# A gated cross-attention kernel: the preparation of its first attention becomes a stream of the timetable, and the loads are put in order of first use

## The chip, the core and the metric

The kernel runs on one core of a Trainium2 chip. The core has a matrix engine (TensorE, PE in the profile, with PEld for its weight loads), a vector engine (VectorE, DVE), a scalar engine (ScalarE, ACT), a general engine (GpSimd, POOL) and a sync engine (SyncE, SP) that here only starts DMA transfers. Each engine runs its own queue of instructions in order; engines wait for one another through semaphores. SBUF is the on-chip memory with 128 partitions, and PSUM is the memory of eight banks that TensorE writes to. The metric is device time in microseconds, lower is better.

## The reference

The input x has 16 batches of 256 tokens of 128 numbers, and the context has 64 tokens of 128 numbers for each batch. Four blocks follow one another, each added to x with a gate tanh(g):

1. a cross attention of x on the context with 16 heads of 8 numbers, causal, under a padding mask, with weights Wq, Wk, Wv and Wo and no biases;
2. two layers of a local-attention network: token shift, 8 heads of 64, rotary position, windows of 64, then a gated GELU network;
3. a second cross attention with biases and another mask;
4. a mixture of 8 experts with the two best of each token.

```python
x = x + tanh(g_xattn[0]) * L0_xattn(layernorm(x), ctx, ctx, mask_if1, Wq, Wk, Wv, Wo)
x = x + tanh(g_ffn[0])   * L0_ffn(layernorm(x), ...)
x = x + tanh(g_xattn[1]) * L1_xattn(layernorm(x), ctx, ctx, mask_ik0, ...)
x = x + tanh(g_ffn[1])   * L1_ffn(layernorm(x), ...)
# L0_xattn: Q = q @ Wq.T; K = k @ Wk.T; V = v @ Wv.T
# scores = where(causal and mask, Q K^T / sqrt(8), -inf); softmax(scores) @ V @ Wo.T
```

## The kernel before

The kernel holds x in SBUF as `x_sb`, 32 tiles of 128 tokens, two tiles to a batch, and works batch by batch. There are three stages: the first cross attention, the local network with both layers, and the second cross attention together with the experts. Inside a stage the order of instructions on every engine comes from `play`, which follows `timetable`. That function plays through tables of steps such as `CROSS_STEPS`: a row has the step's name, its lag (in which round of the loop a batch reaches it), its engine, an assumed duration, the steps it needs, and the buffers that it takes with the steps that give each back. Several tables can be played together as streams; a stream may wait for a step of another. On each engine a stream's steps keep the order given by lag and table row. The assumed durations only decide the order; on the chip the engines wait for one another through semaphores.

One batch of the first cross attention goes through these steps. DVE takes mean and variance (`stat`, L776), POOL the root and the normalised rows (`rstd`, `apply`, L781 to L794), PE turns the rows (`turn`, L756) and ACT copies them out (L805). PE makes the query (`query`, L854) and ACT copies it to `QT` (L860). POOL spreads the batch's keys by head (`keys`, `Kd`, L841). PE makes the scores (`score`, L869 to L885): a row of mask penalties `pen`, a causal part from `causal_g` and `query_g`, and the products. DVE takes the maxima (`top`, L894) and splits them into three narrow parts (`parts`, L903 to L911), which PE turns (`mturn`, L916). PE makes the scores again with keys on the partitions (`score_t`, L932 to L946) with the maxima subtracted, ACT takes the exponential (L956), PE mixes the values (`mix`, L969), ACT and DVE divide (L978 to L992), PE projects (`project`, L999) and DVE adds to `x_sb` (`add`, L1006). One PSUM bank M serves turn, query, mturn and project; three pairs of banks (BIG0 to BIG2) serve the scores.

Before the stage there is a preparation, written out in program order. Loads: ACT starts the context (512 KB), the eight weight matrices (64 KB each), the two small masks and the router, and SP starts x in four pieces, the gates, the masks spread over all partitions (512 KB each), the four small pieces of `fill_c`, and after these all other weights. The framework hands out eight DMA semaphores in turn to all loads, so a load is issued only when the load eight places earlier in the program has landed, and its engine stands still until then. POOL makes the identity, the constants, the causal mask and the local masks `lmask`, which only the second stage reads, and clears buffers. DVE makes `head_of`, `sel`, 16 copies of the causal mask, 8 copies of the identity (`query_g`) and the penalties. Then `prepare` (L625) turns the four weights, turns the context, makes all keys (L608) and all values (L614) of layer 0, and turns the penalties (L654), in eight PSUM banks of its own (pool `bank_prep`). The stage's pool takes the same banks afterwards, so its first turn (L756) waits until they are given back. The corresponding work for the second cross attention, `rest`, is already a stream: `TABLE_STEPS` from the fourth batch on, `REST_STEPS` at the stage's end.

Of the kernel before, what the change touches and what calls it, by code (L numbers as in the profile page):

```python
# [30 lines left out]
E = 8  # L31
# [8 lines left out]
CROSS_STEPS = """  # L40
stat 0 DVE 0.92 - sm:apply
project 6 PE 0.5 share M:add
mturn 3 PE 0.25 parts M:mturn_out
score 2 PE 1.25 query_out,keys BIG:top0 BIG:top1
exp1 4 ACT 1.08 score_t,exp0
vals 2 POOL 0.32 - V:mix
mturn_out 3 ACT 0.38 mturn mT:score_t
top0 2 DVE 1.2 score
apply 1 POOL 1.02 offset xn:turn
turn 1 PE 0.4 apply M:turn_out  # L50
turn_out 1 ACT 0.38 turn xnT:query
mix 4 PE 1.8 exp0,exp1,vals O:share
log 4 ACT 0.38 mix
rstd 0 POOL 1.03 stat
top1 2 DVE 1.2 score,top0
query 1 PE 0.6 turn_out M:query_out
parts 2 DVE 0.9 top0,top1 mp:mturn
query_out 1 ACT 0.39 query QT:score+score_t
inverse 4 ACT 0.38 log
exp0 3 ACT 1.08 score_t pT:mix  # L60
score_t 3 PE 1.2 mturn_out,query_out,keys BIG:exp0 BIG:exp1
offset 0 DVE 0.16 rstd
add 5 DVE 0.48 project
refine 4 DVE 0.84 inverse
keys 1 POOL 0.6 - Kd:score+score_t
share 4 DVE 0.43 refine oT:project
# [55 lines left out]

REST_STEPS = """
vals_out1 1 DVE 0.7 vals1
vals0 2 PE 0.98 wturn_out BIG:vals_out0
bo_out 1 DVE 0.25 bo
rw_out 0 DVE 0.2 rw
vals_out0 3 DVE 0.7 vals0
vals_out3 3 DVE 0.7 vals3
cols_out 0 DVE 0.35 cols  # L130
keys_out0 0 DVE 0.75 keys0,cols_out
rw 0 PE 0.15 - BIG:rw_out
vals_out2 0 DVE 0.7 vals2
wturn 0 PE 0.6 - BIG:wturn_out
cols 0 PE 0.15 - BIG:cols_out
keys_out1 3 DVE 0.75 keys1,cols_out
keys0 0 PE 0.95 wturn_out BIG:keys_out0
vals2 0 PE 0.98 wturn_out BIG:vals_out2
bo 0 PE 0.4 bias,wturn_out BIG:bo_out
vals1 0 PE 0.98 wturn_out BIG:vals_out1  # L140
keys1 5 PE 0.95 wturn_out BIG:keys_out1
wturn_out 1 ACT 0.62 wturn
vals3 4 PE 0.98 wturn_out BIG:vals_out3
bias 0 DVE 0.25 cols_out
# [3 lines left out]
seen 7 DVE 1.0 -  # L148
fill 6 DVE 1.2 -
tab0 3 DVE 0.5 -  # L150
tab1 0 DVE 0.5 -
tab3 2 DVE 0.5 -
tab2 1 DVE 0.5 -
# [131 lines left out]
def timetable(streams, room):  # L285
# [26 lines left out]
    def can_go(k, name, b, engine, now):  # L312
# [5 lines left out]
        for j, n in [(k, n) for n in needs] + across.get(name, []):  # L318
            span = streams[j][5]
            if b < span.start:  # L320
                continue
# [59 lines left out]
def flamingo_kernel(ctx: ExitStack, tc: tile.TileContext, a: dict, out: bass.AP):  # L381
# [30 lines left out]
    for i in range(4):  # L412
        nc.scalar.dma_start(w_nat[:, i, :], a[NATS[i]])
# [18 lines left out]
    for g in range(4):  # L432
        nc.sync.dma_start(fill_c[32 * g : 32 * g + 3, :], a["fill_parts"])
# [1186 lines left out]
```

## Time and profile before

| | us |
|---|---|
| median of 3 runs | 1177.72 (1176.37 to 1178.03) |
| the profiled execution | 1179.12 |
| its span, first to last instruction | 1177.2 |
| busy PE / PEld | 1086.2 / 787.4 |
| busy DVE / ACT / POOL | 941.4 / 730.9 / 631.4 |
| first stage, until the last PSUM copy of its steps ends (DVE, L692) | 155.4 |
| mean granted TensorE clock | 0.982 |

The span is what the profiler saw between the first and the last instruction; the execution took 1.9 us more. A row of instructions reads: start, duration of the group, engine, line, operation, out<-in and shapes, count, and in brackets how long the engine stood idle before and what released it. The chain of waits is followed back from the last instruction, and names for each stretch the engine and line that it hung on. The granted clock is the share of full speed at which TensorE was allowed to run. Lines are those of the kernel before; the changed file has other numbers.

### The profile page before, as it was taken

How to read it: one execution, taken by the hardware profiler on the slowest of the kernel's cores; microseconds unless marked ns; L12 is line 12 of the kernel's file. 1: busy time of each engine (PE TensorE's matmuls, PEld its weight loads, DVE VectorE, ACT ScalarE, POOL GpSimd, SP SyncE). 2: the span in 40 equal slices, each digit the busy share in tenths (PEclk: the TensorE clock that was granted, in tenths of full speed). 3: DMA queues.
4: the chain of work that ended last, by engine and by line, in shares of the span. 5: the costliest groups of instructions: out<-in, count | busy, mean ns of one | idle time of the engine just before them, and what ended most of it. 6: DMA issues, size and time to landing. Idle time of an engine off the chain costs nothing.

```text
span 1177.2 us, 28295 instructions
## 1 busy us (share of the span) xinstructions
PE 1086.2 (92%) x11264; PEld 787.4 (67%) x11264; DVE 941.4 (80%) x2103; ACT 730.9 (62%) x1408; POOL 631.4 (54%) x1079
## 2 busy tenths in 40 slices
PE   5899968999999999988999999999979999999997
PEld 3555535677677777755767766777645557999996
DVE  5787678999999956669999999856667884777777
ACT  1455526888888873346888888863326657455552
POOL 4344158999988852338888888833344551111110
PEclk9899989999999999999999999999999999999999
DMA  6300001111111100001111111100000000000000
GB/s 193 126 3 2 3 14 37 37 29 37 29 38 38 27 17 14 1 0 37 38 37 30 37 37 29 33 11 1 1 1 2 2 2 2 12 13 12 13 12 17
DMA packets 29516, 30.02 MB, mean 26 GB/s; under 512 B 4484, under 2 KB 22344, under 8 KB 29384
## 3 DMA queue, kind: packets, MB, share of 16 engines
q1 hardware_dynamic: 27112, 27.15, 9.1%
q8 instruction: 89, 1.46, 0.5%
q10 hardware_dynamic: 2272, 1.06, 0.3%
q14 instruction: 43, 0.35, 0.1%
HBM read 9.33 MB, written 2.10 MB: 10 GB/s over the span
## 4 chain that ended last, share of the span: by engine, by line
PE 71%; DVE 16%; ACT 6%; issue 4%; POOL 1%; DVEq 0%; ACTq 0%; POOLq 0%
PE QK L1121 8%; PE e_y L1508 7%; PE e_h_ps L1486 7%; PE po L969 5%; PE Ag L1375 4%; PE OB L1281 4%; PE TR L1269 4%; PE SC L1228 3%; PE VB L1151 3%; PE OB L1299 3%; PE TR L1200 3%; ACT pr L1251 3%; PE sT L946 3%; DVE mx L1237 3%; PE sc L885 2%
## 5 line engine op out<-in xcount | busy, mean ns | idle before, releaser
L1251 ACT ACTIVATE pr<-SC,mx,rn 128x128 f32<-128x128 f32 x512 | 185.5, 468 | 35.9 <-DVE mx L1242 35.8
L1121 PE MATMUL QK<-wqkv,hbuf 128*128 128x512 f32 x256 | 130.9, 635 | 19.7 <-DVE qn L1132 14.9
L1264 POOL TENSOR_TENSOR pr<-pr,rs 128x1024 f32<-128x1024 f32 x64 | 121.3, 1896 | 14.6 <-DVE rs L1259 11.4
L1516 DVE SCALAR_TENSOR_TENSOR x_sb<-e_y,e_comb,x_sb 128x128 f32<-128x128 f32 x256 | 89.1, 349 | 21.6 <-PE e_y L1508 13.7
L1498 ACT ACTIVATE e_h<-e_h_ps 128x1024 f32<-128x1024 f32 x48 | 49.2, 1025 | 77.2 <-PE e_y L1508 61.8
L1121 PEld LDWEIGHTS QK<-wqkv,hbuf 128*128 128x128 f32 x256 | 44.6, 193 | 78.1 <-issue 42.1
L894 DVE TENSOR_REDUCE nm<-sc 128x16 f32<-128x1024 f32 x64 | 74.7, 1210 | 21.6 <-PE sc L885 21.5
L1508 PE MATMUL e_y<-mw,e_h 128*128 128x128 f32 x768 | 91.8, 277 | 0.0
L1486 PE MATMUL e_h_ps<-e_xnT,mw 128*128 128x256 f32 x384 | 89.8, 383 | 0.3
L1508 PEld LDWEIGHTS e_y<-mw,e_h 128*128 128x128 f32 x768 | 89.2, 192 | 0.7
L1166 POOL TENSOR_TENSOR qn<-qn,u 128x512 f32<-128x512 f32 x64 | 81.3, 1271 | 10.5 <-DVE qn L1132 7.9
L1132 DVE TENSOR_TENSOR u<-QK,tab 128x1024 f32<-128x1024 f32 x64 | 76.8, 1200 | 10.6 <-ACT sq L1129 5.2
L1129 ACT ACTIVATE sq<-QK 128x1024 f32<-128x1024 f32 x64 | 65.9, 1030 | 29.7 <-DVE u L1132 9.3
L1258 DVE TENSOR_REDUCE rs<-pr 128x8 f32<-128x1024 f32 x64 | 77.5, 1211 | 7.9 <-ACT pr L1251 5.3
L1237 DVE TENSOR_REDUCE mx<-SC 128x8 f32<-128x1024 f32 x64 | 77.6, 1212 | 6.4 <-PE SC L1228 6.4
L1167 POOL TENSOR_TENSOR qn<-qn,u 128x512 f32<-128x512 f32 x64 | 81.6, 1275 | 0.0
L956 ACT ACTIVATE xpT<-sT,penT 128x1024 f32<-128x1024 f32 x64 | 69.5, 1114 | 19.0 <-PE sT L946 19.0
L1272 ACT COPY pT<-TR 128x1024 f32<-128x1024 f32 x64 | 64.4, 1007 | 24.1 <-PE TR L1269 24.1
L1132 DVE TENSOR_TENSOR qn<-QK,tab 128x1024 f32<-128x1024 f32 x64 | 77.6, 1213 | 1.1 <-ACT sq L1129 1.1
L1146 DVE TENSOR_REDUCE ss<-sq 128x16 f32<-128x1024 f32 x64 | 77.1, 1205 | 1.1 <-ACT sq L1129 1.1
L1486 PEld LDWEIGHTS e_h_ps<-e_xnT,mw 128*128 128x128 f32 x384 | 70.3, 190 | 10.9 <-DVE x_sb L1516 2.7
L1385 ACT ACTIVATE hhg<-Ag,cols 128x256 f32<-128x256 f32 x64 | 28.7, 472 | 72.8 <-PE Ag L1375 36.4
(215 smaller groups left out, 2648.0 us busy)
## 6 DMA issues: line engine op xcount, KB each, us to landing
vbuf<-vbuf SPq DMA_DIRECT2D x96, 128.0 KB
hbuf<-yT SPq DMA_DIRECT2D x32, 64.0 KB
out_dram<-x_sb SPq DMA_DIRECT2D x32, 64.0 KB
hbuf<-yT SPq DMA_DIRECT2D x32, 63.8 KB
wqkv<-in_L_ffn_wqkv_dram SPq DMA_DIRECT2D x2, 768.0 KB
mw<-in_L_ffn_w_dram SPq DMA_DIRECT2D x2, 768.0 KB
x_sb<-in_x_dram SPq DMA_DIRECT2D x2, 640.0 KB
w<-in_L_ffn_w_dram SPq DMA_DIRECT2D x2, 341.0 KB
```

What stands on the lines that cost most here:

```text
L1121: nc.tensor.matmul(ps[:, 512 * j : 512 * j + 512], lhsT=hbuf[b % 3][:, W + t * P : W + (t + 1) * P], rhs=wqkv[:, l, 512 * j : 512 * j + 51 ...
L1132: nc.vector.tensor_tensor(work(tag, b, t, [P, 2, LH, LD], 2, wp), live["QK", b, t].rearrange("p (q h d) -> p q h d", q=2, h=LH), tab[:, l, ...
L1146: nc.vector.tensor_reduce(ss, live["sq", b, t].rearrange("p (g d) -> p g d", d=LD), AX.X, ALU.add)
L1166: nc.gpsimd.tensor_add(qg[:, :, 0:32], qg[:, :, 0:32], ug[:, :, 32:64])
L1167: nc.gpsimd.tensor_add(qg[:, :, 32:64], qg[:, :, 32:64], ug[:, :, 0:32])
L1237: nc.vector.tensor_reduce(mx, live["SC", b, t].rearrange("p (g c) -> p g c", c=P), AX.X, ALU.max, negate=True,)
L1251: nc.scalar.activation(pr[:, g, :], live["SC", b, t][:, g * P : (g + 1) * P], AF.Exp, bias=live["mx", b, t][:, g : g + 1], scale=live["rn" ...
L1258: nc.vector.tensor_reduce(rs, live["pr", b, t], AX.X, ALU.add)
L1264: nc.gpsimd.tensor_tensor(pr, pr, rs, ALU.mult)
L1486: nc.tensor.matmul(ps[:, c * S : (c + 1) * S], lhsT=mw1[:, (4 * j + c) * P : (4 * j + c + 1) * P], rhs=live["xnT", b], start=True, stop=True,)
L1508: nc.tensor.matmul(y[:, e * D : (e + 1) * D], lhsT=live["h", b][:, c, t * P : (t + 1) * P], rhs=mw2[:, c, :], start=(c == cs[0]), stop=(c ...
L1516: nc.vector.scalar_tensor_tensor(xt, live[f"y{t}", b][:, e * D : (e + 1) * D], live["comb", b][:, t, e : e + 1], xt, ALU.mult, ALU.add,)
```

## The change

`prepare` becomes a table, `FIRST_STEPS`, with a function for each step, and is played together with the batches of the first cross attention in the same PSUM pool: its steps use the three BIG pairs and the bank O. Steps of the batches get a list of needs on it (`needs`); a third entry gives the batch from which a need holds, for which `can_go` gets two new lines. Rows on engines named LW, LC, LX, LM, LN, LP, LA and LD stand for loads and constants with an assumed time of landing and issue nothing. Weights are turned in pairs, Wk with Wq and Wv with Wo, for which the list `NATS` and the indices of Wq and Wv change. `CROSS_STEPS` keeps its steps and durations but has other lags and another order of rows.

The loads are in another order and other pieces. ACT starts only Wk, the context in two halves, and Wq. SP starts x in pieces of 2, 2, 4, 6, 8 and 10 tiles, the wide mask of the first attention in one piece for two batches and one for fourteen, the other weights, the small masks, and the rest as before. In program order of the built kernel SP's queue is: x of batch 0, the two gates, `parts_in`, the mask of batches 0 and 1, x of batch 1, Wv, the two small masks, x of batches 2 and 3, the rest of the mask, Wo, and then the remaining x, the other mask, the weights of layer 1 and the router. The four small loads into `fill_c` become one load of six numbers to every partition and three small DVE steps (`part`). The copies of the causal mask become 8 of twice the width on DVE (`late`), those of the identity go to ACT (`unit`), and the penalties are made by two wider instructions instead of four.

The local masks move from POOL's start into four steps `local0` to `local3` of `TABLE_STEPS`, after the fourth batch has begun its scores. `TABLE_STEPS` and `REST_STEPS` get new lags and row order.

In the built program the order of TensorE from the query of batch 2 to the stage's end is the old one, apart from the turn of the router weights, which moves three steps towards the end, and the last keys and values, which change places. Before that, TensorE's order is: Wk and Wq turned, both halves of the context, Wv and Wo, keys 0, batch 0 turned, values 0, query 0, penalties, values 1, scores 0, batch 1 turned, values 2, query 1, keys 1, values 3, mturn 0, scores 1. On DVE the add now stands ahead of the offset of the norm, and one table step at a time stands between `parts` and the add.

```diff
+FIRST_STEPS = """
+vals_out1 8 DVE 0.7 vals1
+wturn_out1 4 ACT 0.38 wturn1
...
+wload0 3 LW 5.0 -
+wload1 6 LW 2.6 wload0
+wturn0 0 PE 0.8 wload0 BIG:wturn_out0
+wturn1 4 PE 0.4 wload1 BIG:wturn_out1
+cturn0 0 PE 1.0 cload0 BIG:cturn_out0+cdup0
+cturn1 1 PE 0.7 cload1 BIG:cturn_out1+cdup1
+keys0 4 PE 1.7 wturn_out0,cturn_out0 BIG:keys_out0
+vals0 4 PE 1.1 wturn_out1,cdup0 BIG:vals_out0
+unit 6 ACT 1.6 narrow
+part 2 DVE 0.55 dve
+late 2 DVE 2.0 pool
+mload0 4 LM 5.0 -
...
@@ TABLE_STEPS
-seen 7 DVE 1.0 -
-fill 6 DVE 1.2 -
+seen 0 DVE 1.0 -
+local0 1 POOL 0.98 -
+fill 0 DVE 1.2 -
+local3 3 POOL 0.8 -
...
@@ timetable: can_go
-        for j, n in [(k, n) for n in needs] + across.get(name, []):
+        for j, n, *since_b in [(k, n) for n in needs] + across.get(name, []):
             span = streams[j][5]
-            if b < span.start:
+            if b < max(span.start, *since_b, 0):
                 continue
...
@@ loads
-    nc.scalar.dma_start(
-        ctx_nat, a["ctx_1024"].rearrange("b k d -> (b k) d").rearrange("(t p) d -> p t d", p=P)
-    )
-    nc.sync.dma_start(x_sb[:, 0:4, :], x_in[:, 0:4, :])
+    ctx_in = a["ctx_1024"].rearrange("b k d -> (b k) d").rearrange("(t p) d -> p t d", p=P)
     NATS = [
-        "L0_xattn_Wk", "L0_xattn_Wv", "L0_xattn_Wq", "L0_xattn_Wo",
-        "L1_xattn_Wk", "L1_xattn_Wv", "L1_xattn_Wq", "L1_xattn_Wfc",
+        "L0_xattn_Wk", "L0_xattn_Wq", "L0_xattn_Wv", "L0_xattn_Wo",
+        "L1_xattn_Wk", "L1_xattn_Wq", "L1_xattn_Wv", "L1_xattn_Wfc",
     ]
-    for i in range(4):
-        nc.scalar.dma_start(w_nat[:, i, :], a[NATS[i]])
+    def load_weight(q, i):
+        q.dma_start(w_nat[:, i, :], a[NATS[i]])
+    def load_x(lo, hi):
+        nc.sync.dma_start(x_sb[:, lo:hi, :], x_in[:, lo:hi, :])
+    def load_mask(i, n, lo, hi):
+        nc.sync.dma_start(
+            mask_i[:, i, SK * lo : SK * hi],
+            a[n][lo:hi].rearrange("b k -> (b k)").unsqueeze(0).partition_broadcast(P),
+        )
+    load_weight(nc.scalar, 0)
+    load_x(0, 2)
+    nc.scalar.dma_start(ctx_nat[:, 0:4, :], ctx_in[:, 0:4, :])
     nc.sync.dma_start(g_raw[:, 0:2], a["g_xattn"].unsqueeze(0).partition_broadcast(P))
+    load_weight(nc.scalar, 1)
     nc.sync.dma_start(g_raw[:, 2:4], a["g_ffn"].unsqueeze(0).partition_broadcast(P))
-    mask_n = prep.tile([B, 2, SK], I32, tag="mask_n", name="mask_n")
+    nc.sync.dma_start(
+        parts_in.rearrange("p r i -> p (r i)"),
+        a["fill_parts"].rearrange("r i -> (r i)").unsqueeze(0).partition_broadcast(P),
+    )
+    load_mask(0, "mask_BxS2_if1", 0, 2)
+    nc.scalar.dma_start(ctx_nat[:, 4:8, :], ctx_in[:, 4:8, :])
+    load_x(2, 4)
+    load_weight(nc.sync, 2)
     for i, n in enumerate(("mask_BxS2_if1", "mask_BxS2_ik0")):
-        nc.scalar.dma_start(mask_n[:, i, :], a[n])
-    mask_i = prep.tile([P, 2, B * SK], I32, tag="mask_i", name="mask_i")
-    fill_c = prep.tile([P, 2], F32, tag="fill_c", name="fill_c")
-    nc.vector.memset(fill_c, 0.0)
-    def load_mask(i, n):
-        nc.sync.dma_start(
-            mask_i[:, i, :],
-            a[n].rearrange("b k -> (b k)").unsqueeze(0).partition_broadcast(P),
-        )
-    load_mask(0, "mask_BxS2_if1")
-    for g in range(4):
-        nc.sync.dma_start(fill_c[32 * g : 32 * g + 3, :], a["fill_parts"])
-    for lo, hi in ((4, 12), (12, 22), (22, 32)):
-        nc.sync.dma_start(x_sb[:, lo:hi, :], x_in[:, lo:hi, :])
-    load_mask(1, "mask_BxS2_ik0")
+        nc.sync.dma_start(mask_n[:, i, :], a[n])
+    load_x(4, 8)
+    load_mask(0, "mask_BxS2_if1", 2, B)
+    load_weight(nc.sync, 3)
+    for lo, hi in ((8, 14), (14, 22), (22, 32)):
+        load_x(lo, hi)
+    load_mask(1, "mask_BxS2_ik0", 0, B)
     for i in range(4, 8):
-        nc.scalar.dma_start(w_nat[:, i, :], a[NATS[i]])
-    rw_nat = prep.tile([E, D], F32, tag="rw_nat", name="rw_nat")
-    nc.scalar.dma_start(rw_nat, a["L1_ffn_router_w"])
+        load_weight(nc.sync, i)
+    nc.sync.dma_start(rw_nat, a["L1_ffn_router_w"])
...
@@ constants, masks
-    for g in range(4):
-        for i in range(2):
-            to, of = slice(32 * g, 32 * g + 32), slice(32 * i, 32 * i + 32)
-            for u in range(2):
-                nc.vector.tensor_copy(causal_g[to, i, u, :], causal[of, :])
-            nc.vector.tensor_copy(query_g[to, i, :], ident_bf[of, :])
...
+    def local_mask(i):
+        if i == 0:
+            nc.gpsimd.memset(lmask, 0.0)
+        first, half = i // 2, i % 2
+        part = lmask[64 * half : 64 * half + 64, first, :]
+        nc.gpsimd.affine_select(
+            out=part, in_=part, compare_op=ALU.is_ge, fill=lfill,
+            base=0, pattern=[[1, P]], channel_multiplier=-1,
+        )
+        nc.gpsimd.affine_select(
+            out=part, in_=part, compare_op=ALU.is_ge, fill=lfill,
+            base=W, pattern=[[-1, P]], channel_multiplier=1,
+        )
...
@@ prepare
+    def prepare(pp):
...
+        def wturn(_, j, home):
+            turn_weights(2 * j, 2, acc(f"wT{j}", home))
+
+        def wturn_out(_, j):
+            turned_weights(2 * j, 2, live[f"wT{j}"])
+
...
+        def part(_, j):
+            one = prep.tile([P, 3], F32, tag="one", name="one")
+            nc.vector.tensor_reduce(
+                one, ident.rearrange("p (g r) -> p r g", g=4)[:, 0:3, :], AX.X, ALU.add
+            )
+            own = prep.tile([P, 2, 3], F32, tag="own", name="own")
+            nc.vector.tensor_tensor(
+                own, parts_in.rearrange("p r i -> p i r"),
+                one.unsqueeze(1).to_broadcast([P, 2, 3]), ALU.mult,
+            )
+            nc.vector.tensor_reduce(fill_c, own, AX.X, ALU.add)
+        def fill(_, j):
+            fill_rows(0, 2 * j, (2, B)[j])
+        def late(_, j):
+            for g in range(4):
+                for i in range(2):
+                    to, of = slice(32 * g, 32 * g + 32), slice(32 * i, 32 * i + 32)
+                    nc.vector.tensor_copy(
+                        causal_g[to, i], causal[of, :].unsqueeze(1).to_broadcast([32, 2, SK])
+                    )
+        def unit(_, j):
+            for g in range(4):
+                for i in range(2):
+                    to, of = slice(32 * g, 32 * g + 32), slice(32 * i, 32 * i + 32)
+                    nc.scalar.copy(query_g[to, i, :], ident_bf[of, :])
...
-    with tc.tile_pool(name="bank_prep", bufs=8, space=bass.MemoryType.PSUM) as pp:
-        prepare(lambda name: pp.tile([P, 512], F32, tag="bank", name=name))
...
-        Wq, Wo = wT[:, 4 * layer + 2, :], wT[:, 4 * layer + 3, :]
+        Wq, Wo = wT[:, 4 * layer + 1, :], wT[:, 4 * layer + 3, :]
...
@@ first cross attention
+        needs = dict(
+            stat=[(1, "xload0"), (1, "xload1", 1)], rstd=[(1, "pool")], query=[(1, "wturn_out0")],
+            keys=[(1, "heads"), (1, "keys_out0"), (1, "keys_out1", B // 2)],
+            score=[(1, "fill0"), (1, "fill1", 2), (1, "late"), (1, "unit")],
+            mturn=[(1, "narrow")], score_t=[(1, "sels")], exp0=[(1, "pturn_out")],
+            vals=[(1, f"vals_out{j}", 4 * j) for j in range(4)],
+            project=[(1, "wturn_out1")], add=[(1, "gates")],
+        )
+        homes = lambda r, b: accs + ("O",)
+        before = (FIRST_STEPS, {}, None, {}, homes, range(1))
         tables = (TABLE_STEPS, {}, (0, "score", 3), {}, anywhere, range(1))
-        keys = dict(keys_out0=[(1, "seen")], keys_out1=[(1, "seen")])
+        keys = dict(keys_out0=[(2, "seen")], keys_out1=[(2, "seen")])
         others = (REST_STEPS, keys, (0, "score", B - 1), {}, anywhere, range(1))
         homes = lambda r, b: (dict(hn="exn", VB="M")[r],)
         norms = (NORM_STEPS, dict(stat=[(0, "add")]), None, {}, homes, range(EARLY))
         play(
-            [xattn, tables, others, norms], CROSS_ROOM,
-            [cross(0, *pools), later, later, first(*pools, "e_xn", "M")],
+            [(CROSS_STEPS, needs, *xattn[2:]), before, tables, others, norms], CROSS_ROOM,
+            [
+                cross(0, *pools), prepare(pools[2]), later, later,
+                first(*pools, "e_xn", "M"),
+            ],
         )
```

## The prediction

> **What bounds the kernel now.** I read the page's slices first, then the busy times by stretch, the waits of the first 31 us, the instructions in order of time there, and the chain of waits.
>
> Slices (40 of 29.4 us, busy tenths, then the granted clock of TensorE):
>
> ```profile
> PE   5899968999999999988999999999979999999997
> ACT  1455526888888873346888888863326657455552
> PEclk9899989999999999999999999999999999999999
> ```
>
> TensorE is the bound almost everywhere; the thin slices are the start (5 of 10) and the handover to the next stage (6, slice six). By stretch (busy us per engine with counts, granted clock, DMA share, GB/s):
>
> ```profile
> core 0: us, PE busy (x) PEld busy (x) DVE busy (x) ACT busy (x) POOL busy (x), PEclk, DMA share, GB/s
> 0.00:25.18 25.18, 12.93 (x66) 8.65 (x67) 12.63 (x59) 4.86 (x9) 12.54 (x51) 1.00 0.62 183
> 25.18:40.00 14.82, 12.05 (x99) 6.31 (x99) 8.20 (x24) 4.25 (x8) 4.98 (x11) 0.54 0.92 320
> 40.00:52.84 12.84, 12.10 (x208) 7.18 (x207) 10.46 (x31) 6.56 (x14) 3.85 (x8) 1.00 0.01 3
> 52.84:133.18 80.34, 73.99 (x1218) 44.41 (x1215) 64.86 (x191) 42.67 (x78) 32.24 (x72) 1.00 0.01 2
> ```
>
> The first 25 us are half empty on every engine; the next 15 run at half clock; then TensorE is 92 to 94% busy. So the start is a latency chain, and what follows is not. Waits up to 31 us (total, times, longest):
>
> ```profile
> ACT L564 <- DMA w_nat<-in_L_xattn_Wv_dram: 11.9, 1, 11.9
> ACT xnT L805 <- PE xnT_ps L756: 7.4, 2, 4.7
> PE KT_ps L608 <- ACT ctxT L641: 3.5, 1, 3.5
> ```
>
> ACT does nothing before 11.88: its queue carries 12 load issues that wait for earlier loads. In order of time:
>
> ```profile
> 11.88 1.28 ACT L564 ACT_TABLE_LOAD   x1 [11.88 <-DMA w_nat<-in_L_xattn_Wv_dram]
> 14.40 3.78 PE L608 MATMUL KT_ps<-ctxT,wT 128*128 128x512 f32 x4 [3.54 <-ACT ctxT L641]
> 17.97 4.07 PE L614 MATMUL V_ps<-wT,ctxT 128*128 128x128 f32 x32
> 23.02 0.41 PE L756 MATMUL xnT_ps<-ident,xn 128*128 128x128 f32 x2 [0.74 <-POOL Kd L841]
> 27.14 2.35 DVE L894 TENSOR_REDUCE nm<-sc 128x16 f32<-128x1024 f32 x2 [4.27 <-PE sc L885]
> ```
>
> Batch 0 is turned (23.02) only after all keys, values and the penalty transpose. The chain then has mT (L916) of batches 0 to 3 at 30.65, 38.80, 45.83 and 54.13, and from there one batch per 7.24 us:
>
> ```profile
> 60.15 0.66 PE pw L999 x4
> 60.80 0.03 issue
> 60.83 0.49 DVE x_sb L1006
> 61.32 0.04 issue
> 61.37 0.27 PE mT_ps L916 x2
> ```
>
> **The change part by part.** From mT of batch 3 on, TensorE's order is the old one, so I compare that landmark.
>
> *Loads.* ACT keeps 4 issues, none of which waits: 0.72 + 4 x 0.5 = 2.7, table load 1.28, free at 4.0 instead of 13.2. The others go to SP. Before, x (256 KB) and the context (512 KB) had landed by 5.71, when the issue of Wo behind them went out. The new first 768 KB (x of batch 0, Wk, Wq, the context) should land by about 6.0, with the small broadcasts. Seven issues stand before Wo on SP, each waiting for the load eight places back; from Wk's landing (3.8, interpolated between issue and 6.0) at 0.45 each, Wo is issued at 7.0. Wo took 5.71 to 8.67 = 2.96, so 10.0 is the estimate, its own earlier row being the nearest; bounds 9.5 (the second small mask, issued at 6.56, let its reader go at 9.10: 2.54) and 14.0 (the four fill issues of before went out over 4.12 us, 1.03 each: seven such from 3.8, then 2.96).
>
> *TensorE up to the first scores.* The new order is two weights, the context, Wv and Wo, the first keys, batch 0 turned, values 0, query 0, penalties, values 1, scores 0. So everything waits for Wo. The transposes are on at 6 to 7, beside the wait. From 10.0: last transpose 0.2, keys 3.78/2 = 1.9 (half-clock price), turn 0.4, values 0 at half clock 4 tiles x 0.45 = 1.8, query 1.2 (L854 took 1.22 at 28.15), penalties 0.3, values 1 at full clock 4.07/4 = 1.0, scores 0.39 + 0.39 + 1.03 merged to 1.44 as at 54.34: 18.2. Before, the first reduction of scores began at 27.14; now 18.3: **8.8** earlier.
>
> *Other queues to the same point.* DVE: three memsets and the ident steps end at 2.3, then `part` waits for its small broadcast (6.2; at most 8.0, when SP's third fill issue shows the gates' broadcast in, and then all below moves by 1.8); stat 0.92, eight causal copies, twice as wide as the 0.168 of before (1.4 to 2.7, taken 1.6, since those are mostly fixed cost), offset, stat, the two context copies 0.64 each, small fills, offset, stat, penalties 0.6, values 0 (after 14.3) 0.7, the rest of the fill 0.65, stat 0.92, values 1 0.7: 17.9. That is only 0.4 behind TensorE, so the next delay is there. ACT: copies end 13.0, eight query copies, between DVE's 0.18 for them and ACT's 0.37 for four times the size (taken 0.22, its smallest row), end at 14.4 to 16.0 and QT by 16.4: hidden under values 1 (to 16.8) either way. POOL: without the local masks (memset, eight selects, memset: to 6.3 among others) the memsets end near 5; xn 0 at 9.8, xn 1 at 12.5, Kd at 13.2: hidden. The masks reappear after Kd of batch 4, 3.3 us in a period where POOL has 32.24 of 80.34 us busy: cost 0, and if that cover went, at most 3.3.
>
> *Scores to mT 0.* Before 3.51 us, all DVE, with TensorE empty. Now TensorE does turn 1, values 2, query 1, keys 1 and values 3 there: 0.4 + 1.0 + 1.1 (with ACT's copy) + 0.9 + 1.0 = 4.4 from 18.2. mT 0 at 22.6 against 30.65: gain **8.05**, 0.75 given back.
>
> *mT 0 to mT 1.* Before 8.15 at half clock (scores 2.69, query 1.22, scores_t 2.8). At full clock scores end 0.3 + 1.44 later, then reduction and parts 3.46 and 0.1: 5.3; one values copy (0.7) on DVE fits before. Gain **2.85**. mT 1 to mT 3 (7.03 + 8.30) hang on the exps and was at full clock: 0, though the exp table load now lies in the open for up to 0.3.
>
> *The rest.* DVE's add stands before the offset, and one fill or table step stands between parts and add. Before, DVE waited 0.62 to 0.84 us for the projection behind the same steps: 0 (cadence rival below). Router and keys trade places at the stage's end: +-0.2. The second cross attention only takes other weight indices: 0.
>
> Sum: 8.05 + 2.85 = 10.9. The profiled execution is 1179.12 (span 1177.2 and 1.9 around), so 1168.2; that execution is 1.4 above the median of 1177.72, hence 1166.8, and I say **1167**.
>
> **The rivals.**
> *Loads bind.* For: SP already waited 1.7, 1.6 and 1.3 us at its fill issues. Against: all these loads are small. Each us of Wo beyond 10.0 costs one us: at 14.0 the gain is 6.9, 1171.
> *Only issue time is saved.* If the first uses wait for the same bytes as before, ACT wins just its eight issues fewer at 0.45, 3.6 us: 1174.1. For: bytes land in issue order, 768 KB by 5.71 before and 6.0 now. Against: ACT's 11.9 us was mostly waiting for loads that its first copy does not read. [...]
> *The clock.* For: the rows 25.18 to 40.00 show 0.54, and 162.0 to 172.4, at the next stage's start, 0.51. If the clock opens only after scores 0, values 1 and scores cost 0.8 + 1.25 more, and turn to values 3 up to 2.2: gain 6.6, 1171. An earlier handover also meets the next stage's half-clock stretch elsewhere; one projection of 4 matmuls takes 3.17 to 3.75 there against 1.95: +-2. [...]
> *Slower: the cadence.* If DVE's new order (add behind parts and the inserted steps) makes a batch longer than TensorE's 7.24, twelve periods pay it. DVE's own work is 64.86 over 80.34/7.24 = 11.1 periods, 5.8 each, and 7.3 in the one that gets `seen` and `fill` (0.7 and 0.75). It decides above 7.24 + 10.9/12 = 8.15; at 8.5 the time is 1182. For: that one period. Against: 1.4 us free in the others, and it falls where the exps make it 8.3 long.
> *It does not do what it says:* if the first scores still wait for all preparation, as the old 23.02 did, only ACT's earlier start counts and later waits replace it: no change, 1177.7.
>
> **How the numbers follow.** Likeliest (gain 8 to 14): 0.69, own range 1164 to 1170. Loads bind 0.12; issue time only 0.04; clock 0.08; cadence 0.05; nothing 0.02. The range 1163 to 1172 takes in the first and most of loads and clock, 0.69 + 0.09 + 0.06 = 0.84. Below or above 0.2% (2.4 us, what the measurement can tell): faster 0.93, same 0.02, slower 0.05.
>
> **What would show it.** ACT's table load near 2.7; Wo's transpose near 10; keys right behind it; the first reduction near 18 and mT 0 near 22.6; granted clock 1.00 from about 15 with no half-clock stretch after; mT to mT 5.3, 7.0, 8.3, then 7.24; the stage's last projection 11 us earlier. Wrong if a wait of SP holds Wo past 14, if DVE stands at `part` or the second `fill`, or if the batches' distance is not 7.24.

## The result and the profile after

The changed kernel takes 1168.82 us in the median of 4 executions (1167.82 to 1170.0), the kernel before 1177.05 beside it (1176.18 to 1178.03): a ratio of 0.993, with a 95% interval of 0.9913 to 0.9947. It is faster, and by about 8 us. The profiled execution of after took 1167.82 (span 1166.0), that of before 1179.12 (span 1177.2), so these two differ by 11.3. Why 8 and 11 are both honest numbers is a good part of what follows.

The slices of after (29.2 us each, busy tenths, then the granted clock):

```profile
PE   6999968999999998888999999999979999999997
ACT  3555447888888863357888888853326557555552
PEclk9999989999999999999999999999999999999999
```

The first slice of TensorE is 6 instead of 5, the second 9 instead of 8, ACT's first two slices are 3 and 5 instead of 1 and 4, and the clock's dip has left slice two. By stretch (busy us per engine with counts, granted clock, DMA share, GB/s), cut near the first scores, behind the first batches and behind mT of batch 3, where this list ends:

```profile
0.00:18.00 18.00, 8.66 (x31) 6.14 (x32) 8.66 (x41) 6.65 (x17) 9.17 (x39) 1.00 0.79 230
18.00:32.00 14.00, 12.55 (x171) 8.49 (x173) 11.94 (x34) 6.28 (x12) 7.64 (x17) 1.00 0.51 160
32.00:44.70 12.70, 11.45 (x202) 6.74 (x198) 10.61 (x28) 7.04 (x13) 6.90 (x19) 1.00 0.68 237
```

The second row begins with the first scores. Before, the stretch that held them and the batches behind them (25.18 to 40.00) ran at 0.54 of the clock, and this one runs at 1.00. The 1.00 of the first row says less: the trace holds no record of the clock before 17.76, and two key products take 1.92 us at 12.44 and 1.02 at 21.77 (below). The waits of the first 31 us:

```profile
PE p_wT L652 <- DMA w_nat<-in_L_xattn_Wo_dram: 4.5, 1, 4.5
DVE own L763 <- DMA parts_in<-in_fill_parts_dram: 3.5, 1, 3.5
```

ACT's wait of 11.9 us is gone. TensorE waits 4.5 us for Wo, and DVE stands at `part` for 3.5 us until its small broadcast is there (5.83). In order of time (ACT, SP, PE and DVE):

```profile
2.70 1.28 ACT L655 ACT_TABLE_LOAD   x1 [2.70 <-issue]
...
7.41 0.43 SPq L470 DMA_DIRECT2D w_nat<-in_L_xattn_Wo_dram  x1
...
12.18 0.47 PE L652 MATMUL p_wT<-ident,w_nat 128*128 128x128 f32 x1 [4.48 <-DMA w_nat<-in_L_xattn_Wo_dram]
12.44 1.92 PE L663 MATMUL p_KT<-ctxT,wT 128*128 128x512 f32 x2
14.15 0.63 PE L897 MATMUL xnT_ps<-ident,xn 128*128 128x128 f32 x2
14.58 1.91 PE L669 MATMUL p_V<-wT,ctxT 128*128 128x128 f32 x8
...
20.28 2.35 DVE L1035 TENSOR_REDUCE nm<-sc 128x16 f32<-128x1024 f32 x2 [0.33 <-PE sc L1026]
...
21.77 1.02 PE L663 MATMUL p_KT<-ctxT,wT 128*128 128x512 f32 x2
...
23.79 0.28 PE L1057 MATMUL mT_ps<-ident_bf,mparts 128*128 128x128 bf16 x2
29.04 0.28 PE L1057 MATMUL mT_ps<-ident_bf,mparts 128*128 128x128 bf16 x2 [0.50 <-DVE mparts L1052]
35.71 0.28 PE L1057 MATMUL mT_ps<-ident_bf,mparts 128*128 128x128 bf16 x2
...
44.02 0.27 PE L1057 MATMUL mT_ps<-ident_bf,mparts 128*128 128x128 bf16 x2 [0.58 <-DVE x_sb L1147]
```

The first reduction stands at 20.28 (27.14 before) and mT of batch 3 at 44.02 (54.13 before). From there TensorE's mT of every batch stands 10.11 or 10.12 us earlier than before. Where the 11.2 us between the spans arose is read from four landmarks on TensorE: the last batch's mT of the first stage, the first product with the values in the local stage (OB), the first mT of the second cross-attention, and the end.

| between | before | after | gained |
|---|---|---|---|
| start and last mT of stage one | 139.98 | 129.86 | 10.12 |
| and first OB ("the handover") | 65.12 | 63.97 | 1.15 |
| and first mT of the second cross-attention | 673.13 | 673.67 | -0.54 |
| and the end | 299.02 | 298.54 | 0.48 |

### The profile page after: what moved, and what is told of

It reads as the page before. It is cut to its first block, busy times and chain, and to the rows that moved or that the text cites. A ratio compares the mean times of both kernels' runs of the same rounds, so it can differ in the third digit from the quotient of the medians.

```text
span 1166.0 us, 28276 instructions
## 1 busy us (share of the span) xinstructions
PE 1078.4 (92%) x11264; PEld 785.4 (67%) x11264; DVE 941.0 (81%) x2088; ACT 734.1 (63%) x1417; POOL 634.2 (54%) x1079
## 4 chain that ended last, share of the span: by engine, by line
PE 71%; DVE 16%; ACT 6%; issue 3%; POOL 2%; DMA 1%; SPq 0%; ACTq 0%; DVEq 0%; POOLq 0%
PE QK L1262 8%; PE e_y L1649 7%; PE e_h_ps L1627 7%; PE po L1110 5%; PE Ag L1516 4%; PE OB L1422 4%; PE TR L1410 4%; PE SC L1369 3%; PE TR L1341 3%; PE OB L1440 3%; PE VB L1292 3%; ACT pr L1392 3%; DVE mx L1378 2%; PE sc L1026 2%; PE sT L1087 2%
## 5 line engine op out<-in xcount | busy, mean ns | idle before, releaser
L1657 DVE SCALAR_TENSOR_TENSOR x_sb<-e_y,e_comb,x_sb 128x128 f32<-128x128 f32 x256 | 89.1, 349 | 21.6 <-PE e_y L1649 13.7
L1270 ACT ACTIVATE sq<-QK 128x1024 f32<-128x1024 f32 x64 | 66.0, 1031 | 27.2 <-PE QK L1262 10.2
L1526 ACT ACTIVATE hhg<-Ag,cols 128x256 f32<-128x256 f32 x64 | 28.7, 473 | 72.9 <-DVE hhg L1534 36.7
```

The costliest lines, as they stand in the source:

```text
L1657: nc.vector.scalar_tensor_tensor(xt, live[f"y{t}", b][:, e * D : (e + 1) * D], live["comb", b][:, t, e : e + 1], xt, ALU.mult, ALU.add,)
```

## The experiments

Theory at the outset: the start is a latency chain, the steps played together with the batches shorten it, and what is missing against the forecast (mT of batch 0 at 23.79 instead of 22.6) is Wo, which lands late. Rivals: the order of the loads alone gives the gain; the clock alone gives it; the end is set by something else than the start.

**Wo early.** After, with one load moved on SP's queue:

```diff
     load_x(2, 4)
     load_weight(nc.sync, 2)
+    load_weight(nc.sync, 3)
     for i, n in enumerate(("mask_BxS2_if1", "mask_BxS2_ik0")):
...
     load_mask(0, "mask_BxS2_if1", 2, B)
-    load_weight(nc.sync, 3)
```

> The kernel after, with the load of Wo issued directly behind that of Wv on the same queue, ahead of the small masks, x of batches 2 and 3 and the rest of the first mask. Theory (in the kernel after everything up to the first scores waits for Wo, which is issued at 7.41 and transposed at 12.18): Wo is issued at about 5.5 and transposed at 8 to 9, the keys follow at 9 to 10, and then DVE's own chain (fill part at 5.83, second copy of the context, values) binds, so the first reduction starts at 16.3 to 17.0 against 20.28, mT of batch 0 and with it the whole stage are 3 to 4 us earlier, and the time is 1165 to 1166. Rival (TensorE's chain is held by something else, the copies on ACT or the second half of the context): the first reduction stays within 0.5 us of 20.28 and the time at 1168 to 1169.

SP's queue and TensorE in this kernel, in order of time:

```profile
5.54 0.43 SPq L470 DMA_DIRECT2D w_nat<-in_L_xattn_Wo_dram  x1
...
7.42 0.69 PE L652 MATMUL p_wT<-ident,w_nat 128*128 128x128 f32 x2
7.90 1.92 PE L663 MATMUL p_KT<-ctxT,wT 128*128 128x512 f32 x2
```

Parts of its chain of waits ahead of the first scores:

```profile
2.25 3.88 DMA parts_in<-in_fill_parts_dram
...
10.87 0.60 DVE ctxT L712
11.47 0.08 DVE off L926
11.55 0.09 issue
11.64 0.88 POOL xn L935 x2
12.53 0.58 POOL Kd L982
```

Wv and Wo are turned in one row at 7.42 with no wait between them, at most 2.3 us after Wo's issue; behind the 256 KB of x and 448 KB of mask it had taken 4.72. The keys start at 7.90, 4.54 earlier, and the first reduction at 16.17. The chain no longer passes TensorE there, but the small broadcast `parts_in`, for which DVE stands until 6.23, and behind it DVE's copies and POOL. So this load and DVE's order are the next limit by this chain; no run here moves them. mT of batch 3 is at 39.91: 4.11 earlier. Yet the time is 1167.81 (1163.46 to 1168.99), 1.0 below the median of after (2.5 below its second measurement, further down), and the profiled execution, 1167.21, is 0.6 below that of after. The theory of the start holds (3 to 4 were expected there); the time, expected at 1165 to 1166, does not follow it. The landmarks say where it went: the handover took 67.43 instead of 63.97. The second profile of after, further down, has the same handover of 67.43; beside that one the span with Wo early is 3.8 us shorter (1165.4 and 1169.3).

**The steps without the loads.** After, with the old loads in their old order (here the weights, on ACT's queue again):

```diff
-    load_weight(nc.scalar, 0)
-    load_x(0, 2)
-    nc.scalar.dma_start(ctx_nat[:, 0:4, :], ctx_in[:, 0:4, :])
+    nc.scalar.dma_start(ctx_nat, ctx_in)
+    load_x(0, 4)
+    for i in (0, 2, 1, 3):
+        load_weight(nc.scalar, i)
...
```

> The kernel after, its preparation in steps as it is, but with the loads of the kernel before: the same transfers, on the same queues, in the same order (the fill constants still come in one small load where before had four). Theory (the order of the steps carries most of the gain, and of the loads only the end of ACT's wait matters): ACT is free at about 11.9 and copies from 13.3, the keys start near 14.4 and the first reduction near 22.5 (20.28 after, 27.14 before), mT of batch 3 is near 45.7 (44.02 after, 54.13 before), so about 8.4 of the 10.1 us are kept: 1170 to 1171. Rival (the order of the loads carries the gain): mT of batch 3 within 2 us of 54.13, 1175 to 1177.

ACT waits again, and TensorE waits for ACT:

```profile
10.34 1.28 ACT L649 ACT_TABLE_LOAD   x1 [10.34 <-DMA w_nat<-in_L_xattn_Wk_dram]
...
12.55 2.08 PE L657 MATMUL p_KT<-ctxT,wT 128*128 128x512 f32 x2 [1.85 <-ACT ctxT L702]
```

The keys start at 12.55 and mT of batch 3 stands at 44.50, so 9.6 of the 10.1 us of the first stage are kept (8.4 were expected; ACT was free at 10.34 and not at 11.9). The time is 1171.99 (1170 to 1171 expected), 5 below before, with a handover of 68.11. So the order of the loads in the changed kernel is worth only 0.5 us, because Wo is last among what the keys stand behind. With Wo early it is worth 44.50 - 39.91 = 4.6.

**The loads without the steps.** Before, with the loads of after:

```diff
+    load_weight(nc.scalar, 0)
+    load_x(0, 2)
+    nc.scalar.dma_start(ctx_nat[:, 0:4, :], ctx_in[:, 0:4, :])
...
         prepare(lambda name: pp.tile([P, 512], F32, tag="bank", name=name))
```

> The kernel before, its preparation in program order ahead of the first batch, but with the loads of the kernel after (order, queues, sizes, the fill constants in one small load and two small operations more). Theory (the old order asks for all four weights first, so the keys wait for Wo, which lands last): the four weights are turned near 12.2, the keys start near 14.5 as before (14.40), the first reduction is within 1.5 us of 27.14 and the time within 2 us of 1177. Rival (the loads carry the gain): the first reduction at 22 or earlier, 1170 to 1172.

```profile
12.42 0.47 PE L621 MATMUL wT_ps<-ident,w_nat 128*128 128x128 f32 x1 [3.99 <-DMA w_nat<-in_L_xattn_Wo_dram]
...
21.99 0.41 PE L778 MATMUL xnT_ps<-ident,xn 128*128 128x128 f32 x2 [0.75 <-POOL Kd L863]
```

All four weights are turned at 12.42, the keys start at 13.57, batch 0 is turned at 21.99 behind all keys and values, and mT of batch 3 is 0.83 earlier than before. The time is 1178.10, a ratio of 1.0004 (0.9982 to 1.0026). The loads alone give nothing at the end. The order on SP's queue in the changed kernel is another matter, as Wo's 4.1 us in the first stage show.

**The clock alone.** Before, with four matmuls behind the first scores whose result nobody reads:

```diff
+            if b == 0 and not biased:
+                warm = pp.tile([P, 512], F32, tag="O", name="warm", bufs=1)
+                for _ in range(4):
+                    nc.tensor.matmul(warm, lhsT=wT[:, 0, :], rhs=..., start=True, stop=True)
```

> The kernel before, with four more matmuls of 128x512 on TensorE behind the first scores, whose result nobody reads, to keep TensorE busy while DVE reduces the scores of batch 0. It tells what the half-clock stretch from 25.5 to 39.1 costs by itself. Theory (that stretch is there because TensorE stands idle then, and it costs the 2.85 us between mT of batch 0 and of batch 1): the half-clock stretch is gone or shorter, mT 0 to mT 1 takes 5.3 to 6.0 instead of 8.15, and the time falls by 2 to 3 us. Rival (the distance is set by DVE's reductions or ACT's exps, not by the clock): mT 0 to mT 1 stays at 7.5 or more, and the time falls by less than 1 us. The clock may also stay low if the idle time before the first scores is what closed it; then the stretch is as long as before and nothing is told of its price.

The stretch that had 0.54 of the clock in the kernel before, in this one:

```profile
25.18:40.00 14.82, 12.55 (x146) 6.75 (x142) 9.53 (x26) 5.93 (x10) 5.00 (x11) 1.00 0.93 320
```

mT 0 to mT 1 takes 5.24 instead of 8.15, and mT of batch 3 stands at 51.40: 2.73 earlier. That is the price of the half clock there, as the forecast had it (2.85). But the time is 1179.16, 1.0017 of before (1.0 to 1.0035): nothing is left at the end. The handover took 68.21 here against 65.12; these are single profiles, and the kernel before has 68.16 in its second one. As with Wo early, a gain of the first stage went at the same place, though the instruction order after the first stage is the same.

**The handover.** Between 137 and 200 us the first batches go through the local stage, one QK projection at a time in one PSUM tile, and TensorE has gaps. These are the QK rows of after:

```profile
145.65 1.96 PE L1262 MATMUL QK<-wqkv,hbuf 128*128 128x512 f32 x4 [0.61 <-ACT yT L1171]
151.36 3.42 PE L1262 MATMUL QK<-wqkv,hbuf 128*128 128x512 f32 x4 [0.61 <-DVE qn L1273]
158.34 3.75 PE L1262 MATMUL QK<-wqkv,hbuf 128*128 128x512 f32 x4 [3.55 <-issue]
165.80 1.96 PE L1262 MATMUL QK<-wqkv,hbuf 128*128 128x512 f32 x4 [2.01 <-DVE qn L1273]
```

The same projection takes 1.96 or 3.75, as the clock is 1.00 or 0.50. The half-clock stretches in the profiles of before and after last 3.41, 6.83, 10.24 or 13.65 us, apart from the last of each, which runs past the last instruction. The next four runs test whether their place decides the end. First the changed kernel itself, again:

> The kernel after once more, as it is, in more executions and on the same chip as the three kernels with filled gaps. The traces so far show the first stage shortened by 10.1 us here, 14.2 with Wo early and 2.7 in the kernel before with extra matmuls, and yet 11.3, 11.9 and -0.2 us at the end: the difference arises between 137 and 200 us, where the local stage begins and TensorE's clock is halved for 10.2 to 20.5 us, in pieces that are multiples of 3.41 us. Theory (the end depends on where these windows fall on the same instructions): the time scatters by 2 to 6 us with no change in the first stage. Rival (the time is fixed by the instruction order): all executions within 1 us.

It took 1170.30 (1165.72 to 1171.03 in 6 executions), so the scatter of the theory is there. Its profiled execution took 1171.03, 3.2 more than the first, with the same program and the first stage at the same place (mT of batch 3 at 43.95, the last mT at 129.79). The handover took 67.43 instead of 63.97. By stretch, the first profiled execution of after and then this one:

```profile
150.00:165.00 15.00, 9.53 (x18) 4.36 (x18) 9.40 (x18) 5.27 (x9) 9.55 (x16) 0.66 0.04 9
165.00:180.00 15.00, 12.29 (x108) 7.00 (x109) 13.08 (x15) 8.38 (x19) 13.31 (x25) 1.00 0.16 37
180.00:197.00 17.00, 13.65 (x151) 8.93 (x150) 16.75 (x19) 13.57 (x30) 15.25 (x22) 1.00 0.15 33
```

```profile
150.00:165.00 15.00, 9.92 (x18) 4.33 (x18) 9.05 (x18) 5.07 (x8) 9.47 (x16) 0.54 0.04 9
165.00:180.00 15.00, 12.40 (x104) 6.50 (x104) 11.56 (x13) 8.32 (x21) 11.65 (x23) 0.89 0.16 37
180.00:197.00 17.00, 13.42 (x115) 8.41 (x116) 16.24 (x18) 11.61 (x26) 13.73 (x20) 0.90 0.14 32
```

The first OB row of each, at which the handover ends:

```profile
193.83 1.15 PE L1422 MATMUL OB<-pT,vbuf 128*64 128x64 f32 x32
```

```profile
197.22 1.15 PE L1422 MATMUL OB<-pT,vbuf 128*64 128x64 f32 x32
```

Then the gaps are filled, in three kernels:

```diff
 def qk(b, t):
...
+            idle = {(0, 0): 2, (0, 1): 3, (1, 0): 3}.get((b, t), 0) if l == 0 else 0
+            if idle:
+                warm = pp.tile([P, 512], F32, tag="OB", name=f"warm{b}_{t}", bufs=1)
+                for _ in range(idle):
+                    nc.tensor.matmul(warm, lhsT=wqkv[:, l, 0:P], rhs=wqkv[:, l, 0:512], ...)
```

> The kernel after, with 2, 3 and 3 more matmuls of 128x512 behind the first three QK projections of the local stage, into a bank whose first reader comes 30 us later; nobody reads them. They fill gaps in which TensorE waits for DVE and ACT. Theory (the half-clock stretches at the start of the local stage come from these gaps, and cost what the three projections and eight transposes there take above their price at full clock: 1.46 + 1.77 + 0.87 = 4.1 us, of which some lies beside DVE): no half-clock stretch between 146 and 166 us, the projections take 1.96 each, and the time falls by 2 to 4 us, to 1165 to 1167, with less scatter. Rival (DVE and ACT set the pace of the handover, so the clock costs nothing): no change, or up to 2 us longer for the added matmuls.

> Wo early (as in the run with Wo's load behind Wv's) and the same filled gaps. Theory (the 4.11 us won in the first stage were given back to the half clock at the start of the local stage, 20.5 us of it against 10.2): with the gaps filled the 4.1 us stay, so the time is 3.5 to 4.5 us below the kernel after with filled gaps: 1161 to 1163. Rival (what was given back is a wait for something else, like the masks or a load): the two filled kernels differ by less than 1 us.

> The kernel before with the same filled gaps. It tells what the change is worth when the start of the local stage runs at full clock in both kernels. Theory (the change's own gain is the 10.12 us of the first stage, and the 11.3 of the two profiled executions and the 8.2 of the medians both hold a piece of the clock's luck): the kernel before falls by 2 to 5 us too, to 1172 to 1175, and the filled kernels differ by 10.1 +- 0.5 us. Rival (the new order of the local masks or of the norms changes the handover itself): the difference is under 9 or over 11.5.

The QK rows of after with filled gaps, in order of time:

```profile
144.84 1.95 PE L1262 MATMUL QK<-wqkv,hbuf 128*128 128x512 f32 x4 [0.61 <-ACT yT L1171]
146.63 1.88 PE L1272 MATMUL warm<-wqkv 128*128 128x512 f32 x4
150.55 1.98 PE L1262 MATMUL QK<-wqkv,hbuf 128*128 128x512 f32 x4 [0.61 <-DVE qn L1281]
152.37 2.74 PE L1272 MATMUL warm<-wqkv 128*128 128x512 f32 x6
156.09 1.96 PE L1262 MATMUL QK<-wqkv,hbuf 128*128 128x512 f32 x4 [0.97 <-issue]
```

With 7.4 us of useless work more on TensorE, the changed kernel takes 1166.83 against 1170.30 on the same chip, the one with Wo early 1162.27 (1160.91 to 1164.65), and the kernel before 1174.59 against 1178.17. (Wo early without filled gaps, 1167.81, ran on another chip.) The half-clock stretch between 146 and 166 us is gone, as expected; the scatter is hardly less (4.5 us against 5.3). The profiled execution of after with filled gaps is its slowest, 1170.13: its handover took 64.13, but from the first mT of the second cross-attention to the end it took 301.70 instead of 298.54, with 20.5 us at half clock around its start, from 859.1 on. So time won in the handover can go at the next such place. The handovers of all traces, by how long the clock was halved in them:

| at half clock, us | handover, us | runs |
|---|---|---|
| 0 | 62.31 to 62.47 | before filled (twice), Wo early filled |
| 3.4 | 64.13, 64.14 | after filled, and the last kernel below |
| 10.2 | 63.97, 65.09 | after; loads without steps |
| 13.7 | 65.12 | before |
| 17.1 | 68.11 to 68.21 | steps without loads, before with the clock kept, before again |
| 20.5 | 67.43 to 67.48 | Wo early, after again, masks first |

So in these profiles the handover takes 62.4 at full clock and up to 5.8 more, and the length of the stretches alone does not set it (68.11 to 68.21 with 17.1 us of them, 67.43 to 67.48 with 20.5). With the gaps filled, Wo early is worth 4.56 us at the end (1166.83 - 1162.27), where 3.5 to 4.5 were expected; its last mT of the first stage is 4.1 us ahead of that of after and 3.3 ahead of that of after with filled gaps. The rival with another wait, by which the two differ by less than 1 us, falls.

The two filled kernels without Wo early differ by 7.8 in the median, not by 10.1. In the letter this is the rival of the last expectation, but not by its cause: the handovers at full clock are 62.31 and 62.47, whichever order the masks have. The rest lies in the first stage of the kernel before. Its profile was taken twice more:

> The kernel before, profiled once more. The forecast took the half-clock stretch from 25.5 to 39.1 and the 8.15 us between mT of batch 0 and of batch 1 as a property of the kernel. In its executions without a trace the mean clock runs from 0.980 to 0.989 beside times from 1182 to 1174; 13.65 us at half clock are 0.006 of the mean. Theory (in a part of the executions that stretch isn't there, because the windows fall otherwise): where the mean clock is 0.988 or more, mT 0 to mT 1 takes about 5.3 and mT of batch 3 stands near 51.3; where it is 0.986 or less, 8.15 and 54.1. Rival (the stretch is always there, and the scatter comes from later stages alone): 8.15 and 54.1 in either.

> The kernel before with the filled gaps, profiled once more. Of its eleven executions so far four have a mean clock of 0.993 or 0.994 and take 1172.3 to 1173.3, the others 0.982 to 0.991 and 1174.4 to 1177.5; the traced one (1175.52, 0.989) has 13.65 us at half clock in the first stage, from 28.6, and about 7 at the very end. A mean of 0.994 leaves room for about 14 us in all. Theory (the half-clock stretch of the first stage is not in every execution of the kernel before): a trace with a mean of 0.993 or more has no stretch of 13.65 there, mT of batch 0 to mT of batch 1 takes about 5.3 and mT of batch 3 stands near 51.5. Rival (it is always there and what varies is later): 8.15 and about 54.4 whatever the mean. A trace with a mean under 0.992 decides nothing.

The kernel before alone came out at 1182.85 with a mean clock of 0.980, a stretch from 28.7, 8.15 from mT 0 to mT 1 and mT of batch 3 at 54.67, as theory and rival both have it for such an execution. With filled gaps it came out at 0.993. These are the mT rows of the first and of the second profile of before with filled gaps:

```profile
29.43 0.39 PE L916 MATMUL mT_ps<-ident_bf,mparts 128*128 128x128 bf16 x2 [2.07 <-DVE mparts L911]
37.58 0.39 PE L916 MATMUL mT_ps<-ident_bf,mparts 128*128 128x128 bf16 x2
...
54.45 0.27 PE L916 MATMUL mT_ps<-ident_bf,mparts 128*128 128x128 bf16 x2 [0.58 <-DVE x_sb L1006]
```

```profile
29.61 0.40 PE L916 MATMUL mT_ps<-ident_bf,mparts 128*128 128x128 bf16 x2 [2.07 <-DVE mparts L911]
36.16 0.28 PE L916 MATMUL mT_ps<-ident_bf,mparts 128*128 128x128 bf16 x2 [0.51 <-DVE mparts L911]
...
51.13 0.27 PE L916 MATMUL mT_ps<-ident_bf,mparts 128*128 128x128 bf16 x2 [0.58 <-DVE x_sb L1006]
```

Same program, the same mT 0 within 0.2, and 3.3 us less at mT of batch 3: mT 0 to mT 1 takes 6.55 instead of 8.15, and the stretch at half clock was 3.41 us instead of 13.65. The last mT of the first stage stands at 140.30 and at 136.97, against 129.05 in after with filled gaps: 11.3 us with the long stretch, 7.9 with the short one. The whole 19 executions of before with filled gaps have a median of 1174.38, 7.55 above after with filled gaps. Which share of executions has the long stretch stays open; four profiles of the old preparation without extra matmuls in the first stage had it, one had a quarter of it.

**The local masks.** After, with `local_mask(0)` to `local_mask(3)` called where before made them, and empty steps in the table:

> The kernel after with the local masks made where the kernel before makes them, in one go at the head of GpSimd's queue, and empty steps in their place beside the cross-attention. It tells what the second half of the change is worth by itself. Theory (the masks hide in both places, since TensorE waits for Wo until 12.18 anyway and the turn of batch 0 follows the keys at 14.15): the first normalised x is 2 to 3.5 us later on GpSimd, mT of batch 0 within 0.5 us of 23.79 and mT of batch 3 within 0.5 of 44.02. Rival (the masks hold up batch 0): mT of batch 0 and all behind it 1 us later or more.

The first normalised x is at 9.42 on POOL instead of 8.78 (2 to 3.5 later was expected), and mT of batch 0 at 23.16 (23.79 and 23.73 in the profiles of after), mT of batch 3 at 43.39. That is a little earlier, not later, but after with filled gaps, whose first stage is that of after, has mT of batch 0 at 22.98; the clock's first record is at 16.0 there and at 16.1 here, and at 17.8 and 17.1 in the profiles of after. The masks cost nothing in the first stage at either place. One execution took 1170.17, with a handover of 67.48.

**A version that beats both.** Wo early with filled gaps is that version: 1162.27, 0.987 of before (0.9849 to 0.989), and 8.0 below after on the same chip. One more try, filling the start of the second cross-attention as well:

```diff
 def score(b, _, *homes):
...
+            if biased and b == 0:
+                warm = pp.tile([P, 512], F32, tag="O", name="warm", bufs=1)
+                for _ in range(3):
+                    nc.tensor.matmul(warm, lhsT=wT[:, 4, :], rhs=..., start=True, stop=True)
```

> Wo early, the filled gaps at the start of the local stage, and three more matmuls that nobody reads behind the first scores of the second cross-attention, where the kernel with Wo early and filled gaps still had 6.83 us at half clock from 860.8 and scattered from 1160.9 to 1164.7. Theory (that scatter is the clock at the start of the second cross-attention): the slower executions go, 1160 to 1161 with a scatter under 1.5 us. Rival (DVE's reductions pace the start of that stage, or the extra matmuls cost what they save): 1162 and the old scatter, or up to 2 us more.

It took 1162.82 (1161.43 to 1163.99), on another chip than the 1162.27. The time from the first mT of the second cross-attention to the end fell from 299.03 to 297.23, with 5.3 instead of 11.6 us at half clock, but the local stage and its handover lost 2.2 and 1.7, with 3.4 us at half clock each where there had been none. The theory's place gained its 1.8 us in these two profiles, but the median did not; whether the scatter (2.6 us against 3.7) became smaller can't be told from six executions each.

## Why the prediction was right

The forecast was 1167, the median 1168.82, inside the range of 1163 to 1172 and of the likeliest case's own 1164 to 1170. By its steps:

- *Loads.* ACT's table load was forecast near 2.7 and stands at 2.70. Wo was issued at 7.41 (7.0), in part by chance: Wk had landed by 2.9 and not at 3.8, but SP then stood 1.3 us for the first half of the context, which landed at 5.07. Wo landed at 12.13 and not at 10.0, though within the bounds of 9.5 to 14.0. This is the term that was mis-sized: the nearest row, Wo's own 2.96 us, came from a queue with less ahead of it. The new place has 704 KB right in front, and Wo took 4.72. The profile of before has a row for a load with much in front (shown below the list): Wq's 64 KB, issued at 2.40 behind the context, let TensorE go at 8.18, 5.8 us later.
- *TensorE up to the first scores.* From Wo's transpose to the first reduction 8.3 were forecast (10.0 to 18.3), and 8.10 were taken (12.18 to 20.28). The sum has values 0 at half clock and values 1 and the scores at full clock, which the forecast expected from about 15 on; no run shows what sets that moment. The trace of after has its first record of the clock, at full speed, at 17.8, and the keys began 2.2 us later than forecast (12.44 and not 10.2): values 0 took 1.91, the query 1.06, values 1 1.22 (1.8, 1.2 and 1.0 forecast).
- *Other queues.* DVE waited 0.33 for the first scores, against 0.4 forecast, so it was indeed the next limit; Wo early showed it. ACT's eight `unit` copies took 2.50 and were hidden, within the forecast 1.4 to 3.0.
- *Scores to mT 0.* The turn, values 2, query 1, keys 1 and values 3 ended in time, and 0.75 was not given back: 20.28 to 23.79 is 3.51, the same as before. mT 0 is thus at 22.6 + 2.1 - 0.2 - 0.7 = 23.8, as measured: 6.86 gained and not 8.05.
- *mT 0 to mT 1.* 5.25 (5.3 forecast). mT 1 to mT 2 took 6.67 instead of 7.03, a gain of 0.36 that was not forecast; mT 2 to mT 3 8.31, then 7.24 per batch. The cadence rival did not come.
- *Sum of the first stage.* 10.12 (10.9 forecast). Two profiles of after agree to 0.1; that of after with filled gaps ends this stage 0.8 earlier.
- *The rest, costed at 0.* Here +1.15, -0.54 and +0.48 came in. The handover has 10.2 us at half clock instead of 13.7 and the last part 8.2 instead of 11.7; the local stage has 3.4 in both, so its -0.54 stays unexplained. The forecast had this as +-2 inside the clock rival; the handover alone moves by 5.8.
- *The shift to the median* (1.4) stood on three executions. It was the weak place: the profile of before stood 1.4 above its median and that of after 1.0 below its own, so 11.3 between the profiles are 8.2 between the medians, where the forecast had 10.9. The 2.85 us for the clock in the first stage are paid by executions that have that stretch, and the profiled one had it whole (mT 0 to mT 1 took 8.15 with 13.65 us at half clock, 6.55 with 3.41, and 5.24 at full clock with the extra matmuls). In the medians of the filled kernels the change is worth 7.8 us on one chip and 7.6 over all executions. That the forecast came within 2 us is thus in part luck; the second measurement of after, 1170.30, is inside the range but above 1170.
- *Rivals.* "Loads bind" is half of what happened: 2.1 us of it. "Only issue time is saved" is refuted as the cause by the steps without the loads, which keep 9.6 of 10.1 us though ACT waits 10.34 us again.
- *Signs of being wrong.* One of them came: DVE stood at `part`, for 3.5 us until 5.83. The sum had this wait already, until 6.2, and DVE was still the first to be ready for the scores, so it cost nothing here; the sign was badly chosen. "No half-clock stretch after" held for the first stage alone.

Wq's rows in the kernel before:

```profile
2.40 0.45 ACTq L413 DMA_DIRECT2D w_nat<-in_L_xattn_Wq_dram  x1
...
8.18 0.97 PE L599 MATMUL wT_ps<-ident,w_nat 128*128 128x128 f32 x2 [1.10 <-DMA w_nat<-in_L_xattn_Wq_dram]
```

## What to carry to other kernels

When a chain of loads and short steps sets the start, first order the steps so that the first batch asks only for what it reads, and then look which single load stands last among them; here the order of steps gave 9.6 us, the loads by themselves 0.8 in the first stage and nothing at the end, and one load moved ahead of two large ones 4.1 more. Follow a gain by landmarks to the next stage with gaps: here 3.46 of the 4.11 us that Wo early won in the first stage over the first profile of after were gone behind the handover, which had 20.5 us at half clock instead of 10.2, and with eight matmuls that nobody reads in its gaps 4.56 us stood at the end. Compare two profiled executions only after comparing where their half-clock stretches lie.

## What was not expected of the hardware

More work on TensorE made three kernels faster by 3.5 to 5.5 us, the last figure across two chips: eight matmuls of 128x512 that nobody reads (7.4 us) kept the clock at 1.00 from 150 to 165 us (160 to 175 in the kernel before), where it had been 0.54 to 0.66. One program took from 1165.72 to 1171.03 us in ten executions, and the time follows the mean clock: in 63 executions of the kernel before, those at 0.988 or 0.989 took 1173.7 to 1177.4, those at 0.980 1181.1 to 1183.2, and those at 0.982 anything from 1177.9 to 1183.0. A load of 64 KB took 4.72 us from issue to landing behind 704 KB on its queue, and at most 2.3 when it was issued ahead of them.
